# A reordered opening of an attention-plus-experts kernel: sequence 0 first on every engine, masked k by ScalarE, matmuls on the identity

## The chip, the cores and the metric

The kernel runs on one core of a Trainium2 chip. The metric is the device time of one execution in microseconds, the median of several executions. TensorE is called PE here, VectorE DVE, ScalarE ACT, GpSimd POOL and SyncE SP; SP only issues DMAs in this kernel.

## The reference

The input `x` is 32 sequences of 256 tokens with 128 features, all float32. One layer is computed:

```python
xn  = layernorm(x)                                   # no weight, no bias
qkv = (xn @ Wqkv.T)                                  # 16 heads of 8 features
q, k = rope(q), rope(k)
s   = q @ k.T / sqrt(8); s[not (j <= i and i - j <= 64)] = -inf
y   = softmax(s) @ v;  attn = y @ Wproj.T + bproj
g   = xn @ gate_w.T + gate_b; the two highest of 8 experts, softmax over the two
ffn = sum over the two of weight * (gelu(xn @ w1[e] + b1[e]) @ w2[e] + b2[e])
out = x + attn + ffn
```

## The kernel before, in words

**Units.** The 8192 tokens are 16 units of 512 tokens (`NU`); a unit is two sequences, four tiles of 128 tokens. A sequence has the number z, 0 to 31. `norm(u)` (line 259) takes a unit to its normalised rows `xn` (DVE statistics, a power of -0.5 on POOL at line 274, scaling on ACT at 283), its transposed form `xnT` (PE at 290, copied by ACT at 291) and its gate scores (PE at 295, DVE at 299).

**Rotary q and k.** `project(u, t)` (line 543) multiplies `xnT` by the weights of q (t = 0) or k (t = 1) on PE (549), and then DVE shuffles the product (558) and multiplies it by a cosine (565). The shuffled copy is multiplied by a sine, on DVE where `alone` is set (562) and on POOL otherwise (564). `sum` (569) adds the two. Since a head has only 8 features, the score matmuls work on masked copies: `km` and `qm` hold, for each of four slots, only the rows of one head in four, and zeros elsewhere. `alone(z, t)` (574) fills the copy of sequence z by four DMAs, one a slot, 32 KB each. The zeros come from `clear(n)` (499), three sets of buffers for z modulo 3; set 0 is cleared by POOL, sets 1 and 2 by ACT.

**Rounds.** The attention (`run`, line 787) goes through 32 sequences with four rounds each; "round 2.1" is round 1 of sequence 2. In a round, `high` computes scores of sequence z once (mask matmuls at 622, score matmuls at 634) and DVE takes their row maxima (648). `less` computes scores of an earlier sequence with the maxima taken off (PE at 689 and 703), and ACT exponentiates them (713). Either uses one PSUM tile, `sh` or `sl`, so the next round's `high` waits for the maximum of this one. Only `high` works in rounds 0.0 to 1.1, since `less` follows one and a half sequences behind. The four maxima of a sequence go through `parts` (659 to 662), PE (672) and ACT (677) into the rows that `less` takes off.

**Work beside.** At the end of each round `turn` advances the generator `beside` (1037) once. It hands out pieces of norms of later units, of the routing (`route`, four groups of four units, which needs the norms of its group) and of `blocks`, and it issues two scatters a turn (an indirect DMA by POOL at 457, 128 in all) of normalised rows to their experts once a group is routed. When the last scatter is out, all 71 expert blocks run in one piece (lines 909 to 1005), and the rest of the attention follows, with the experts' results added.

**Order.** The schedule is manual: each engine executes its instructions in the order in which the program issues them. SP's DMAs stand in one queue too.

**Opening.** Ahead of round 0.0, lines 868 to 906 do the norm and the projections of unit 0 by halves (half 0 is sequence 0, half 1 is sequence 1), then `weights_late` (232: transposed Wproj, the sum b2 + bproj, and its DMA to `b2_d` at 237), free the pool of raw weights (`raw.close()`, 898) and begin the norm of unit 1. `loads_late` (182) puts the loads of units 2 to 15 on SP in one go. The first act of `beside` is a memset of the tile `void` (1041) in the memory that the raw weights had, and its DMA of 910 KB (1101).

Of the kernel before, what the change touches and what calls it, by code (L numbers as in the profile page):

```python
# [11 lines left out]
F32 = mybir.dt.float32  # L12
I32 = mybir.dt.int32
BF16 = mybir.dt.bfloat16
AF = mybir.ActivationFunctionType
# [4 lines left out]
P = 128  # L20
# [3 lines left out]
T = 256  # L24
# [10 lines left out]
HB = 64  # L35
# [3 lines left out]

C_COS = 0  # L40
C_SIN = 256
C_MQ = 512
C_MK = 768
C_PICK = 960
C_PRE = 1216
C_TIE = 1344
C_NUM = 1352
C_BASE = 1360
C_RUN = C_BASE + NE
C_BLK = C_RUN + 17 * NE  # L50
C_ROW = C_BLK + NB
# [5 lines left out]
def constants():  # L57

    f = np.float32
    c = np.zeros((P, C_ALL), f)  # L60
    p = np.arange(P)
    e = np.arange(NE)
    c[:, C_PRE : C_PRE + P] = p[:, None] < p[None, :]
    c[:, C_TIE : C_TIE + NE] = NE - e
    c[:, C_NUM : C_NUM + NE] = e
    c[:, C_BLK : C_BLK + NB] = np.arange(NB)
    c[:, C_ROW : C_ROW + 128] = p[:, None] + P * np.arange(128)[None, :]
    c[:, C_BASE : C_BASE + NE] = ER * e
# [24 lines left out]
    return c, np.zeros((P, 2 * P), f)  # L93
# [3 lines left out]
def tile_layer(  # L97
# [16 lines left out]
    nc = tc.nc  # L114
# [61 lines left out]
    nc.sync.dma_start(out=wqkv_n, in_=wqkv.rearrange("(t p) c -> p t c", p=P))  # L176
    nc.sync.dma_start(out=c[:, 0:C_MQ], in_=cst[:, 0:C_MQ])
    load_x(0, slice(2, 4))
    nc.sync.dma_start(out=c[:, C_MQ:C_ALL], in_=cst[:, C_MQ:C_ALL])
    load_x(1)  # L180

    def loads_late():
        nc.sync.dma_start(out=wproj_n, in_=wproj)
        load_x(2)
        nc.sync.dma_start(out=b1_n, in_=b1)
        for u in range(3, NU):
            load_x(u)

# [25 lines left out]
    def weights(misc):  # L214

        pw = misc("pw")
        for t in range(3):
            nc.tensor.transpose(pw[:, t * D : (t + 1) * D], wqkv_n[:, t, :], ident)
        nc.vector.tensor_copy(wT[:, 2, :], pw[:, 2 * D : 3 * D])
        for t in range(2):  # L220

            natural = pw[:, t * D : (t + 1) * D].rearrange(
                "p (i s d) -> p i d s", i=4, s=4
            )
            nc.vector.tensor_copy(
                wT[:, t, :].rearrange("p (i d s) -> p i d s", i=4, d=HD), natural
            )
        pw2 = misc("pw2")
        nc.tensor.matmul(pw2[:, 0:NE], lhsT=gw_n, rhs=ident[0:NE, 0:NE], start=True, stop=True)
        nc.vector.tensor_copy(gwT, pw2[:, 0:NE])  # L230
# [16 lines left out]
    def masks():  # L247
        nc.vector.tensor_copy(
            mq, c[:, C_MQ : C_MQ + 4 * HB].rearrange("p (n k) -> p n k", n=2)
        )  # L250
        nc.vector.tensor_copy(unit2[0:HB, :], ident[0:HB, 0:HB])
        nc.vector.tensor_copy(unit2[HB:P, :], ident[HB:P, HB:P])
        nc.vector.tensor_copy(unit, ident)
        nc.vector.tensor_copy(
            pick_i, c[0:NR, C_PICK : C_PICK + 4 * HB].rearrange("p (i k) -> p i k", i=4)
        )
# [217 lines left out]
    class Attention:  # L474
# [4 lines left out]
        def __init__(self, us, pools):  # L479
            self.us = us  # L480
            self.work, self.ps_m, self.ps_y, self.ps_s, fixed = pools
            self.fixed = fixed
            self.vsts, self.kms, self.qms, self.rss = [], [], [], []
            self.qk, self.half = {}, {}
            self.seqs = {}
            self.ended = set()
            self.added = set()
            self.later = []
            self.past = []

# [8 lines left out]
        def clear(self, n):  # L499
# [11 lines left out]
            put(vst.rearrange("p n i o k -> p (n i o k)"), 1.0)  # L511
            self.vsts.append(vst)

            km = fixed.tile([P, 4, HB + T], F32, tag=f"km{n}", name=f"km{n}")
            put(km.rearrange("p s t -> p (s t)"), 0.0)
            self.kms.append(km)
            qm = fixed.tile([P, 4, T], F32, tag=f"qm{n}", name=f"qm{n}")
            put(qm.rearrange("p s t -> p (s t)"), 0.0)
            self.qms.append(qm)
# [54 lines left out]
        def alone(self, z, t, queues=(nc.sync,)):  # L574

            a = self.qk[z // 2, t][:, z % 2, :]
            to = (self.qms, self.kms)[t][z % 3]
            at = HB * t
            for s in range(4):
                queues[s % len(queues)].dma_start(  # L580
                    out=to[s::4, s, at : at + T], in_=a[s::4, :]
                )

        def v(self, z):
# [281 lines left out]


    nc.gpsimd.memset(nhalf, -0.5)
    nc.gpsimd.memset(ones, 1.0)
    att.clear(0)  # L870
    att.clear(1)

    first = [norm(0, 2 * h, 2 * h + 2) for h in range(2)]
    for h in range(2):
        for _ in range(2):
            next(first[h])
        att.flush()
    weights(misc)
    for h in range(2):
        half = slice(h, h + 1)  # L880
        next(first[h])
        next(first[h])
        for t in (1, 0):
            att.project(0, t, half, alone=h == 0)
            att.flush()
            if t or h:
                att.sum(0, t, half)
            if t and h == 0:
                att.alone(0, 1, (nc.sync, nc.scalar))
        if h == 0:  # L890
            att.sum(0, 0, half)
            loads_late()
            masks()
    for g in first:
        for _ in g:
            pass
    weights_late(misc)
    raw.close()
    nc.gpsimd.tensor_copy(
        goes[:, :, :, 0], c[:, C_ROW : C_ROW + 2 * NN].rearrange("p (k n) -> p k n", k=2)  # L900
    )
    second = norm(1)
    for _ in range(3):
        next(second)
    att.flush()
    att.clear(2)


    def experts():
# [126 lines left out]

    def beside():

        rt = early.enter_context(tc.tile_pool(name="rt", bufs=1))
        void = rt.tile([P, NE, 2, ROW], F32, tag="void", name="void")  # L1040
        nc.gpsimd.memset(void, 0.0)
# [65 lines left out]
        u, g, last = 2, 0, False  # L1107
        while next(transfers, transfers) is not transfers:
            z, r = att.now
            if (z, r) == (0, 2):  # L1110
                begin("masks0", att.masks(0))
            if (z, r) == (1, 1):
                begin("masks1", att.masks(1))

# [68 lines left out]
```

## Time and profile before

| | |
|---|---|
| median of 3 runs | 793.06 us (792.67 to 793.94) |
| profiled execution | 838.41 us |
| its span, first to last instruction | 836.6 us |
| mean granted TensorE clock | 0.976 |
| PE busy | 750.3 us of the span (90%) |
| DVE, ACT, POOL busy | 497.0, 381.9, 412.0 us |
| first maximum of round 0.0 starts | 24.62 us |
| maximum of round 2.0 starts | 63.26 us |
| experts | from 395 to about 676 us |

The profiled execution took 45 us longer than the median of the runs. In the timeline a row is: start in us, duration in us, engine, line, operation, output<-input with shapes, and how many instructions were merged; in square brackets stands how long the engine had been idle before it, and what ended that. PEld is the load of weights, which overlaps PE. A "q" behind an engine is its queue, here the issue of a DMA. In the table of stretches each pair is an engine's busy us and its instructions.

### The profile page before, as it was taken

Reading aid. Unit: us, or ns where it says so; the run is one execution under the profiler, and the core shown is the slowest. Engines: PE = TensorE matmul, PEld = TensorE weight load, DVE = VectorE, ACT = ScalarE, POOL = GpSimd, SP = SyncE. Lnnn points to the kernel's source line nnn. Section 1 sums busy time; section 2 is a strip of 40 time slices with the busy share of each in tenths; the row PEclk is TensorE's granted clock in tenths of the full one; section 3 lists DMA queues with packets and bytes.
Section 4 is the critical chain, followed back from the end, with each engine's and each line's share of the span. In section 5 each row is a group of like instructions: output and inputs, shape, how many; then the busy total and the mean of one; then the engine's idle time right before and its main releaser. Section 6 shows DMA issues by size and latency. Waiting matters only on the chain.

```text
span 836.6 us, 20453 instructions
## 1 busy us (share of the span) xinstructions
PE 750.3 (90%) x7524; PEld 483.2 (58%) x7524; DVE 497.0 (59%) x1163; ACT 381.9 (46%) x695; POOL 412.0 (49%) x668
## 2 busy tenths in 40 slices
PE   4899899888888889788999999999999989999985
PEld 2334444444444444333889998999899944444442
DVE  4658867887786687657233333333333348888763
ACT  4346455455455444434434344343344435454552
POOL 2301666477667644664355555555555553634300
PEclk9999999999999999989999999999999999999997
DMA  4600111111111111213677878887778634446100
GB/s 143 179 20 14 46 46 40 46 43 43 49 43 55 50 34 40 96 53 95 199 214 217 224 209 226 227 226 220 219 225 237 198 108 139 137 126 168 41 22 13
DMA packets 126372, 98.87 MB, mean 118 GB/s; under 512 B 14648, under 2 KB 112600, under 8 KB 126272
## 3 DMA queue, kind: packets, MB, share of 16 engines
q1 hardware_dynamic: 117344, 79.64, 34.3%
q0 software_dynamic: 8640, 17.84, 6.1%
q8 instruction: 60, 0.98, 0.5%
q14 instruction: 40, 0.33, 0.1%
q10 hardware_dynamic: 288, 0.08, 0.0%
HBM read 65.09 MB, written 24.02 MB: 107 GB/s over the span
## 4 chain that ended last, share of the span: by engine, by line
PE 63%; ACT 10%; DVE 9%; SPq 7%; issue 6%; DMA 4%; POOL 1%; ACTq 0%; DVEq 0%; POOLq 0%
PE sl L703 10%; PE ph L952 9%; PE po L970 9%; ACT pr L713 9%; PE sl L689 8%; PE sh L634 7%; PE y L725 6%; PE sh L622 5%; DVE mx L648 3%; DMA xg<-xs_d 2%; PE pm L672 2%; PE pk L549 1%; PE pq L549 1%; SPq L932 1%; PE pg L295 1%
## 5 line engine op out<-in xcount | busy, mean ns | idle before, releaser
L713 ACT ACTIVATE pr<-sl 128x1024 f32<-128x1024 f32 x128 | 130.8, 1022 | 232.2 <-PE sh L634 174.2
L648 DVE TENSOR_REDUCE mx<-sh 128x8 f32<-128x1024 f32 x128 | 156.3, 1221 | 106.0 <-PE sh L634 84.7
L981 POOL DMA_INDIRECT ys_d<-yg,at x142 | 137.3, 967 | 138.8 <-DVE yg L976 105.8
L958 ACT ACTIVATE h<-ph,b_b 128x256 f32<-128x256 f32 x284 | 116.3, 470 | 154.6 <-PE ph L952 141.6
L634 PE MATMUL sh<-km,rq 32*64 32x512 f32 x1024 | 153.4, 661 | 0.0
L457 POOL DMA_INDIRECT xs_d<-xn,slot x128 | 126.5, 988 | 44.3 <-issue 27.4
L703 PE MATMUL sl<-qm,rk 32*64 32x256 f32 (+1 forms) x1280 | 147.0, 502 | 0.0
L970 PEld LDWEIGHTS po<-w,h 128*128 128x128 f32 x1136 | 137.9, 192 | 4.3 <-issue 0.7
L970 PE MATMUL po<-w,h 128*128 128x128 f32 x1136 | 138.3, 275 | 0.6 <-issue 0.6
L952 PE MATMUL ph<-xgT,w 128*128 128x256 f32 x568 | 136.2, 383 | 1.1 <-DVE xgT L940 0.9
L689 PE MATMUL sl<-rs,pick_i 76*64 76x512 bf16 x512 | 81.9, 396 | 49.3 <-ACT pr L713 43.6
L952 PEld LDWEIGHTS ph<-xgT,w 128*128 128x128 f32 x568 | 103.3, 192 | 13.0 <-DVE xgT L940 1.1
L975 DVE TENSOR_TENSOR yg<-po,b 128x256 f32<-128x256 f32 x71 | 30.1, 424 | 112.1 <-PE pxg L938 66.4
L725 PE MATMUL y<-pr,vst 128*32 128x128 f32 (+1 forms) x1536 | 78.7, 331 | 2.8 <-issue 1.6
L689 PEld LDWEIGHTS <-pick_i 76*64 76x64 bf16 x512 | 27.8, 109 | 82.8 <-issue 71.2
L725 PEld LDWEIGHTS y<-pr,vst 128*32 128x32 f32 x1536 | 44.8, 117 | 53.3 <-issue 47.4
L703 PEld LDWEIGHTS sl<-qm,rk 32*64 32x64 f32 x1280 | 48.2, 134 | 39.2 <-issue 31.1
L677 ACT COPY rs<-pm 12x1024 bf16<-12x1024 bf16 x63 | 60.2, 1000 | 8.5 <-PE pm L672 7.9
L622 PE MATMUL sh<-mq,unit 64*64 64x512 bf16 x512 | 54.8, 417 | 3.5 <-DVE mx L648 3.2
L734 DVE STREAM_TRANSPOSE yt<-y 128x512 f32<-128x512 f32 x64 | 45.3, 708 | 10.5 <-PE y L725 9.0
L942 DVE COPY at<-xg 128x4 int32<-128x4 int32 x71 | 13.4, 189 | 62.7 <-issue 48.6
L622 PEld LDWEIGHTS <-unit 64*64 64x64 bf16 x512 | 15.7, 105 | 57.5 <-issue 57.2
(143 smaller groups left out, 840.3 us busy)
## 6 DMA issues: line engine op xcount, KB each, us to landing
w<-in_L_ffn_w_dram SPq DMA_DIRECT2D x142, 256.0 KB
xg<-xs_d SPq DMA_DIRECT2D x71, 130.0 KB
yc<-ys_d SPq DMA_DIRECT2D x32, 256.0 KB
b<-b_d SPq DMA_DIRECT2D x71, 64.0 KB
qm<-rq SPq DMA_DIRECT2D x128, 32.0 KB
out_dram<-x SPq DMA_DIRECT2D x32, 128.0 KB
km<-rk SPq DMA_DIRECT2D x126, 32.0 KB
x<-in_L_attn_x_dram SPq DMA_DIRECT2D x15, 256.0 KB
```

Of the source, the lines that this page charges most:

```text
L457: nc.gpsimd.indirect_dma_start(out=xs_d, out_offset=bass.IndirectOffsetOnAxis(ap=slot[:, n, k : k + 1], axis=0), in_=xns[n // NT][:, n % N ...
L622: nc.tensor.matmul(ps[HB * h : HB * h + HB, ii, :, :], lhsT=unit2[half, :], rhs=mq[half, which, :].unsqueeze(1).to_broadcast([HB, 4, 2 * HB]),
L634: nc.tensor.matmul(ps[HB * h : HB * h + HB, ii, :, :], lhsT=q[r, t * HB : (t + 1) * HB], rhs=km[r, :, t * HB : (t + 2) * HB], start=False, ...
L648: nc.vector.tensor_reduce(mx, ps, AX.X, ALU.max, negate=True)
L689: nc.tensor.matmul(ps[HB * e : HB * e + HB, ii, :, :], lhsT=pick_i[:, 2 * ip + ii, :], rhs=rs[e][:, :, n * P : (n + 1) * P], start=True, s ...
L703: nc.tensor.matmul(ps[HB * e : HB * e + HB, ii, :, lo:hi], lhsT=k[r, kt * HB : (kt + 1) * HB], rhs=qm[r, :, n * P + lo : n * P + hi], star ...
L713: nc.scalar.activation(pr, ps, AF.Exp, scale=1.0 / math.sqrt(HD))
L725: nc.tensor.matmul(py[32 * i : 32 * i + 32, 2 * o : 2 * o + 2, lo:hi], lhsT=self.vsts[z % 3][:, tile_, i, o, :], rhs=q["pr", n, i // 2][:, ...
L952: nc.tensor.matmul(ph[:, j * BT : (j + 1) * BT], lhsT=a[:, (k + j) * P : (k + j + 1) * P], rhs=xT, start=True, stop=True,)
L958: nc.scalar.activation(h[:, k + j, :], ph[:, j * BT : (j + 1) * BT], AF.Gelu, bias=b1_b[:, k + j, b : b + 1],)
L970: nc.tensor.matmul(po[:, n, :], lhsT=h[:, k, n * P : (n + 1) * P], rhs=z[:, k, :], start=(k == 0), stop=(k == NHC - 1),)
L981: nc.gpsimd.indirect_dma_start(out=ys_d, out_offset=bass.IndirectOffsetOnAxis(ap=at[:, n, 0:1], axis=0), in_=y[:, n, :], in_offset=None,)
```

## The change

The opening is cut in two. Ahead of the first round there is only what the scores of round 0.0 need, with the second half of unit 0 as far as its k product; the rest (the second half's q, gates, the norm of unit 1, clears, masks, late weights) becomes `opening()`, the first three turns of `beside`. The masked k of sequence 0 is written by four ACT instructions with a 0-or-1 scale per partition (`alone_first`), no longer by four DMAs, so `km` set 0 is not cleared but for its first 64 columns. Three groups of matmuls on the identity, read as bf16, with unused results are added (11, 3 and 2 of 128x512). The loads of units 2 to 15 go out one a turn from round 0.3 on. The constants come in three pieces, not two.

```diff
-C_MQ = 512
+C_HEAD = 512
+C_MQ = 516
...
+    c[:, C_HEAD : C_HEAD + 4] = (p % 4)[:, None] == np.arange(4)[None, :]
...
     load_x(0, slice(2, 4))
-    nc.sync.dma_start(out=c[:, C_MQ:C_ALL], in_=cst[:, C_MQ:C_ALL])
+    nc.sync.dma_start(out=c[:, C_MQ:C_PICK], in_=cst[:, C_MQ:C_PICK])
     load_x(1)
+    nc.sync.dma_start(out=c[:, C_PICK:C_ALL], in_=cst[:, C_PICK:C_ALL])
+    nc.sync.dma_start(out=wproj_n, in_=wproj)
 
     def loads_late():
-        nc.sync.dma_start(out=wproj_n, in_=wproj)
-        load_x(2)
-        nc.sync.dma_start(out=b1_n, in_=b1)
-        for u in range(3, NU):
+        for u in range(2, NU):
+            yield False
             load_x(u)
+            if u == 2:
+                nc.sync.dma_start(out=b1_n, in_=b1)
...
+        def alone_first(self):
+
+            a = self.qk[0, 1][:, 0, :]
+            for s in range(4):
+                nc.scalar.activation(
+                    self.kms[0][:, s, HB:], a, AF.Identity,
+                    scale=c[:, C_HEAD + s : C_HEAD + s + 1],
+                )
+
+        def warm(self, n, tag="sl"):
+
+            ps = self.ps_s.tile([P, 2, 4, P], F32, tag=tag, name=f"warm{len(self.warmed)}")
+            self.warmed.append(n)
+            some = ident.bitcast(BF16)
+            for k in range(n):
+                nc.tensor.matmul(
+                    ps[:, k % 2, :, :], lhsT=some[:, 0:P],
+                    rhs=some[:, 0:P].unsqueeze(1).to_broadcast([P, 4, P]),
+                    start=True, stop=True, skip_group_check=True,
+                )
...
     nc.gpsimd.memset(nhalf, -0.5)
-    nc.gpsimd.memset(ones, 1.0)
-    att.clear(0)
-    att.clear(1)
+    att.kms.append(fixed.tile([P, 4, HB + T], F32, tag="km0", name="km0"))
+    nc.gpsimd.memset(att.kms[0][:, :, 0:HB], 0.0)
 
     first = [norm(0, 2 * h, 2 * h + 2) for h in range(2)]
+    sides = [slice(h, h + 1) for h in range(2)]
+    att.warm(11)
     for h in range(2):
         for _ in range(2):
             next(first[h])
         att.flush()
+    next(first[0])
     weights(misc)
-    for h in range(2):
-        half = slice(h, h + 1)
-        next(first[h])
-        next(first[h])
-        for t in (1, 0):
-            att.project(0, t, half, alone=h == 0)
-            att.flush()
-            if t or h:
-                att.sum(0, t, half)
-            if t and h == 0:
-                att.alone(0, 1, (nc.sync, nc.scalar))
-        if h == 0:
-            att.sum(0, 0, half)
-            loads_late()
-            masks()
-    for g in first:
-        for _ in g:
+    att.warm(3)
+    next(first[0])
+    next(first[1])
+    att.warm(2)
+    masks()
+    att.clear(0)
+    att.project(0, 1, sides[0], alone=True)
+    att.sum(0, 1, sides[0])
+    next(first[1])
+    att.alone_first()
+    att.project(0, 0, sides[0], alone=True)
+    att.sum(0, 0, sides[0])
+    att.project(0, 1, sides[1])
+    att.flush()
+    second = norm(1)
+
+    def opening():
+
+
+        att.sum(0, 1, sides[1])
+        att.project(0, 0, sides[1])
+        att.clear(1)
+        nc.gpsimd.memset(ones, 1.0)
+        for _ in range(3):
+            next(second)
+        yield
+        att.sum(0, 0, sides[1])
+        weights_gates(misc)
+        for _ in range(2):
+            next(second)
+        for g in first:
+            for _ in g:
+                pass
+        yield
+        masks_late()
+        for _ in att.masks(0):
             pass
-    weights_late(misc)
-    raw.close()
-    nc.gpsimd.tensor_copy(
-        goes[:, :, :, 0], c[:, C_ROW : C_ROW + 2 * NN].rearrange("p (k n) -> p k n", k=2)
-    )
-    second = norm(1)
-    for _ in range(3):
-        next(second)
-    att.flush()
-    att.clear(2)
+        att.clear(2)
+        weights_late(misc)
+        nc.gpsimd.tensor_copy(
+            goes[:, :, :, 0], c[:, C_ROW : C_ROW + 2 * NN].rearrange("p (k n) -> p k n", k=2)
+        )
+        raw.close()
+        yield
...
     def beside():
 
+        yield from opening()
...
-            if (z, r) == (0, 2):
-                begin("masks0", att.masks(0))
+            if (z, r) == (0, 3):
+                begin("loads", loads_late())
```

`weights` is split too: the gate weights move to `weights_gates`, the k part is copied first, and `masks` keeps only what `high` needs (`mq` and the two 64x64 units), the rest moving to `masks_late`.

More of the change, by code (lines that the diff above doesn't have):

```diff
@@ L41 @@
 C_SIN = 256
-C_MQ = 512
[L43 to L48, printed above, removed]
+C_HEAD = 512
+C_MQ = 516
+C_MK = 772
+C_PICK = 964
+C_PRE = 1220
+C_TIE = 1348
+C_NUM = 1356
+C_BASE = 1364
 C_RUN = C_BASE + NE
@@ L218, in weights @@
             nc.tensor.transpose(pw[:, t * D : (t + 1) * D], wqkv_n[:, t, :], ident)
-        nc.vector.tensor_copy(wT[:, 2, :], pw[:, 2 * D : 3 * D])
-        for t in range(2):
+        for t in (1, 0):
             natural = pw[:, t * D : (t + 1) * D].rearrange(
@@ L227, in weights, with weights_gates @@
             )
+        nc.vector.tensor_copy(wT[:, 2, :], pw[:, 2 * D : 3 * D])
+    def weights_gates(misc):
         pw2 = misc("pw2")
@@ L252, in masks, with masks_late @@
         nc.vector.tensor_copy(unit2[HB:P, :], ident[HB:P, HB:P])
+    def masks_late():
         nc.vector.tensor_copy(unit, ident)
@@ L487, in __init__ @@
             self.added = set()
+            self.warmed = []
             self.later = []
@@ L512, in clear @@
             self.vsts.append(vst)
-            km = fixed.tile([P, 4, HB + T], F32, tag=f"km{n}", name=f"km{n}")
-            put(km.rearrange("p s t -> p (s t)"), 0.0)
-            self.kms.append(km)
+            if n > 0:
+                km = fixed.tile([P, 4, HB + T], F32, tag=f"km{n}", name=f"km{n}")
+                put(km.rearrange("p s t -> p (s t)"), 0.0)
+                self.kms.append(km)
             qm = fixed.tile([P, 4, T], F32, tag=f"qm{n}", name=f"qm{n}")
```

## The prediction

> **What bounds the kernel now.** I read first the page (spans, busy shares), then the table of stretches, then the timeline of the first 62 us, because the change touches only the opening and what the opening defers.
>
> ```profile
> span 836.6 us, 20453 instructions
> PE 750.3 (90%) x7524; PEld 483.2 (58%) x7524; DVE 497.0 (59%) x1163; ACT 381.9 (46%) x695; POOL 412.0 (49%) x668
> 0.00:56.00 56.00, 40.94 (x174) 19.91 (x174) 29.41 (x100) 22.62 (x45) 14.21 (x23) 1.00 0.46 127
> 56.00:100.00 44.00, 38.40 (x480) 18.41 (x474) 36.87 (x88) 23.99 (x40) 12.29 (x19) 1.00 0.09 27
> ```
>
> PE does 174 instructions in the first 56 us and 480 in the next 44. The opening is thin, and its PE work is slow as well:
>
> ```profile
> 9.79 0.37 ACT L291 COPY xnT<-pt 128x256 f32<-128x256 f32 x1 [0.57 <-PE pt L290]
> 15.83 0.88 ACT L283 ACTIVATE xn<-x,off,rstd 128x128 f32<-128x128 f32 x2 [5.67 <-DVE off L278]
> 16.38 0.86 PE L290 MATMUL pt<-ident,xn 128*128 128x128 f32 x2 [4.09 <-ACT xn L283]
> 22.37 1.98 PE L634 MATMUL sh<-km,rq 32*64 32x512 f32 x8
> 24.62 1.22 DVE L648 TENSOR_REDUCE mx<-sh 128x8 f32<-128x1024 f32 x1
> 31.17 1.83 POOL L1041 MEMSET void<- 128x2080 f32 x1 [5.27 <-DMA b_d<-b_n]
> 34.26 0.16 DVE L278 SCALAR_TENSOR_TENSOR off<-mv,rstd 128x4 f32<-128x4 f32 x1 [4.52 <-POOL rstd L274]
> 54.21 0.64 PE L622 MATMUL sh<-mq,unit 64*64 64x512 bf16 x4
> 58.15 0.41 PE L622 MATMUL sh<-mq,unit 64*64 64x512 bf16 x4
> 110.48 0.64 PE L622 MATMUL sh<-mq,unit 64*64 64x512 bf16 x4
> ```
>
> The reader is to see three things. Sequence 0's q and k are ready by 14.8 us, but its first scores start at 22.37, since sequence 1's half, the gates and Wproj stand ahead of them on PE and DVE. A POOL memset waits for the DMA of b2 and delays round 0.2. And the same mask matmuls take 0.64 us up to 54 us, 0.41 after 58, 0.64 once more at 110: PE has a slow and a fast clock here that the granted-clock column (1.00) does not show.
>
> The maxima start at 24.62 (round 0.0), 28.52, 36.13, 40.02, 46.11 (1.0), 51.35, 56.56 (1.2), 59.74 and 63.26 (2.0). From there the chain is continuous to the end, so a microsecond gained at 2.0 is gained at the end, unless deferred work takes it back.
>
> **Part 1: the way to the first scores.** The second half of x lands at 6.48, and DVE's statistics end at 7.59, as before. The scale `off` of sequence 0 then goes ahead of the weight copies (before: 8.16), so xn starts at 7.68. Transposes are ready for ACT by about 8.8, its copy of 0.37 ends at 9.2, and k's product takes 1.22 us in the slow rows, 0.70 at the fast ratio (0.41/0.64). DVE's four rotary steps took 11.48 to 13.16, 1.68 us: rk by 11.7. DVE's mask casts (0.29 + 2 x 0.19) lie in its wait for PE. q's steps follow on DVE, another 1.7: 13.3. Masked k: an ACT pass of 128x256 is between 0.37 (the copy above) and 0.61 (0.50 for the 128x128 scaling plus 128 elements at the 0.82 ns of the 128x768 against 128x1280 fills); I take the latter, nearest in form, pipelined at 0.49: 3 x 0.49 + 0.61 = 2.1, done by 13.85. Before, its DMAs were issued at 13.2, but nobody was waiting for them: PE's order was. Scores start at **13.85** instead of 22.37: **-8.5**.
>
> The idle matmuls stand ahead of this chain on PE. [...] The last two lie beside ACT's copy. [...]
>
> **The clock.** [...] I take fast up to the first scores, slow from there to 1.2. [...]
>
> **Part 2: the rounds to 1.2, at slow-clock durations.** First maximum at 13.85 + 1.98 + 0.27 = 16.1 (before 24.62).
> - 0.0 to 0.1: DVE has 1.22 + sum 0.4 + shuffle and product 0.8 + unit 1's statistics 1.7 = 4.1 (before 3.9): 20.2.
> - 0.1 to 0.2: unit 1's scaling waits behind the maximum on DVE: 1.9 after it starts, ACT 1.65, last transpose at +4.1, gates 1.71, masks 0.57 and scores 1.98 queued behind them on PE: 8.5. Before it was 7.6, with the b2 stall: that stall goes, and this chain is late in its place: 28.7.
> - 0.2 to 0.3: k of unit 1 2.08 and Wproj 0.47 on PE, then masks and scores: 5.1 (3.9): 33.8.
> - 0.3 to 1.0: v 1.22, gates 1.71, masks and scores: 5.3 (6.1): 39.1.
> - 1.0 to 1.1: 4.1 by PE. But unit 2's statistics now stand on DVE ahead of the maximum, and its load is behind the `void` DMA on SP: b2's DMA, 3.3 us after 0.2's maximum, needs about 2.9 more, then memset 1.83 and fill 0.2, then 910 KB (4.3 us, as at 33.3), then the load: about 13.9 us after maximum 0.2, when DVE wants it at 12.3. I take 4.4: 43.5.
> - 1.1 to 1.2: 5.2 as before: **48.7** against 56.56, **-7.9**.
>
> ACT's clears (3.1) and mask rows (2.6) lie in its idle time. POOL's q product behind the memset isn't due before 1.1.
>
> **Part 3: what comes back.** By the end of round 0.3 the order of the new program has 8 tile statistics where before had 16, so two norms move into sequences 1 and 2. By the end of sequence 2 it has 22 against 20; what it then lacks is the first routing, in sequences 3 and 4 instead of 1 to 3. Scatters start in the middle of sequence 5 (before: 3) and run at 8 a sequence to the same sequence 21; before, there were gaps in sequences 7, 8, 16 and 17. The experts start after 22.0 instead of 21.3: one round more ahead of them, one less behind. Price: sequences 2 and 3 took 14.9 us without scatters, those with scatters 16.9 with norms (183 to 318 us) and 16.9 without (318 to 386). So pieces of norms are nearly free there, and fewer gaps are paid by more rounds without scatters: 3.5 x 15.2 + 16 x 16.9 + 0.75 x 14.5 = 334.5 to the experts, against 332 plus the round more at 3.4 = 335.4. I take +0.5 for the half norm extra, between -1 and +5.
>
> Sum: -7.9 + 0.5 = -7.4 on a span of 836.6, so 829.2 us, or 831.0 for the profiled execution's 838.41. The median is 0.946 of that; scaled, -7.0: **786.0 us**.
>
> **Rivals.**
> [...]
> - **C, the load behind `void` lands late** (b2's DMA took 4.6 us from issue before, against my 2.9, and landing may add 2): 1.1 and 2.0 come some 4 us later, 789.8 us.
> - **D, slower: deferred work returns at full price.** Sequence 2's maxima (63.26 to 73.30) have no wait before them, so DVE is the bound there. Two norms at 2.1 us of DVE (4 x 0.39 + 0.5), 13 routing operations at 0.45 = 5.9 pushed into 3 and 4, and the extra round at 4.2 instead of 3.4: 4.2 + 5.9 + 0.8 = 10.9, less 7.9: +3.0 on the span, 795.9 us. It decides once more than 7.9 us come back, about three quarters of that full price. Against it: the routing's old places are free for the norms.
> - **E, nothing:** the two cancel, 793.
>
> **How the numbers follow.** Chances: mine 0.52, B 0.16, C 0.13, E 0.06, D 0.13. A measurement here can tell 0.2% (1.6 us) from no change. Faster is mine, B and C: 0.81; within 0.2% is E; slower is D. The range must leave out D and may leave out E's upper part: 779.5 (B with 2 us more) to 792.0.
>
> **What would show it.** In the new profile: first scores at 13.9, first maximum at 16.1, 0.2 at 28.7, 1.2 at 48.7, 2.0 at 55.4. Mask matmuls of 0.41 up to 14 us and 0.64 from 0.1 to 1.1 confirm the clock; 0.41 throughout means B. A DVE wait on x<-in_L_attn_x_dram in round 1.0 of 1 to 2 us is mine, of over 4 C. Experts starting less than 5 us earlier means that Part 3 is wrong; not earlier at all is D.

## The result, and the profile after

The changed kernel takes 789.85 us (median of 20 runs, 784.17 to 792.86), the kernel before 793.72 us (20 runs, 790.82 to 803.42). The ratio is 0.9926, with a 95% interval of 0.9904 to 0.9948: 0.74% faster, some 5.9 of 793.7 us. The predicted 786.0 us is a ratio of 0.9911 to the median that it started from, 793.06, and that lies inside the interval.

One thing has to be known before the two profiles are laid side by side: later runs of the same programs fall into two paces, chips on which the kernel before takes 833 to 835 us and chips on which it takes 794 to 796. On which chip the profile before (838.41 us) was taken is not on record, but it has the slower pace, and the profile after (784.24 us, span 782.5) the quicker: the stretch from the maximum of round 6.0 to that of 21.0 takes 252.0 us in the one and 222.6 in the other, and the changed kernel alone takes 255.2 us there on a slow chip (e_after) and 223.0 on a quick one (e_after_b). So the 54 us between the profiles are nearly all the chip's. Rows of the opening can still be compared: e_after and e_after_b reach the maximum of 4.0 at 87.76 and 87.79 us and that of 6.0 at 117.51 and 117.45.

The page and the table of stretches of the changed kernel, with the columns as before:

```profile
span 782.5 us, 20487 instructions
PE 729.0 (93%) x7540; PEld 473.3 (60%) x7540; DVE 500.3 (64%) x1163; ACT 382.8 (49%) x699; POOL 412.7 (53%) x668
0.00:56.00 56.00, 46.39 (x249) 17.90 (x250) 33.22 (x93) 26.95 (x54) 12.63 (x22) 0.70 0.33 94
56.00:100.00 44.00, 40.62 (x502) 20.79 (x500) 38.07 (x94) 24.86 (x42) 6.84 (x6) 1.00 0.19 57
```

PE now does 249 instructions in the first 56 us, 16 of them idle matmuls, where it did 174. The granted clock of that stretch reads 0.70 and no longer 1.00. That isn't a slower clock than before: the mask matmuls below show the same slow clock as before for most of the way. The column is discussed at the end.

The timeline of the opening, the rows that answer to those of before:

```profile
7.57 0.88 ACT L291 ACTIVATE xn<-x,off,rstd 128x128 f32<-128x128 f32 x2 [3.15 <-DVE off L286]
8.36 1.62 DVE L254 CAST mq<-c 128x256 bf16<-128x256 f32 x1
9.29 0.70 PE L559 MATMUL pk<-xnT,wT 128*128 128x256 f32 x2
11.49 0.41 PE L653 MATMUL sh<-mq,unit 64*64 64x512 bf16 x4
12.06 1.70 ACT L598 ACTIVATE km<-rk,c 128x256 f32<-128x256 f32 x4 [1.25 <-DVE rk L581]
13.86 1.93 PE L665 MATMUL sh<-km,rq 32*64 32x512 f32 x8 [1.96 <-ACT km L598]
15.84 1.23 DVE L679 TENSOR_REDUCE mx<-sh 128x8 f32<-128x1024 f32 x1 [1.53 <-PE sh L665]
17.12 0.64 PE L653 MATMUL sh<-mq,unit 64*64 64x512 bf16 x4 [0.18 <-DVE mx L679]
27.77 1.22 DVE L679 TENSOR_REDUCE mx<-sh 128x8 f32<-128x1024 f32 x1 [2.34 <-PE sh L665]
33.77 0.41 PE L653 MATMUL sh<-mq,unit 64*64 64x512 bf16 x4 [0.55 <-DVE mx L679]
34.08 1.83 POOL L1091 MEMSET void<- 128x2080 f32 x1 [2.18 <-DVE pc L690]
42.22 0.29 DVE L276 BATCH_NORM_STATS2 st<-x 128x6 f32<-128x128 f32 x1 [4.14 <-DMA x<-in_L_attn_x_dram]
49.03 0.64 PE L653 MATMUL sh<-mq,unit 64*64 64x512 bf16 x4
53.33 0.41 PE L653 MATMUL sh<-mq,unit 64*64 64x512 bf16 x4
```

The scores start at 13.86, and what they waited for last is `km` of ACT. The memset of `void` no longer waits for the DMA of b2. The clock is fast at 11.49, slow at 17.12, fast in one short stretch around 33.8, slow again, and fast once more by 53. The DVE wait for unit 2's load is 4.14 us.

The starts of the maxima in all runs are below, since nearly every reading rests on them (DVE rows of `mx`, us; "chip" is the pace of the kernel before on the chip):

```text
                      chip  scores  0.0   0.1   0.2   0.3   1.0   1.1   1.2   1.3   2.0  experts
before                 835  22.37  24.62 28.52 36.13 40.02 46.11 51.35 56.56 59.74 63.26  394.4
predicted                   13.85  16.1  20.2  28.7  33.8  39.1  43.5  48.7   -    55.4
after                  794  13.86  15.84 19.79 27.77 32.51 36.27 43.04 47.00 51.74 55.22  354.1
e0_before              835  22.09  24.34 28.23 36.69 40.58 46.67 51.91 57.07 60.24 63.74  398.0
e_after                833  13.89  15.04 18.98 26.96 31.70 36.80 42.33 46.29 49.46 53.56  388.7
e_after_b              796  14.16  16.03 19.98 27.96 32.70 36.46 43.30 47.25 51.99 55.47  354.7
e1_no_idle             835  14.15  15.30 19.24 27.22 31.96 35.02 43.04 47.00 51.74 57.22  389.0
e2_load2               835  13.77  15.33 19.27 27.25 31.99 37.09 40.99 45.95 49.12 53.22  387.9
e2_load2_b             796  14.04  15.27 19.21 27.19 31.93 37.03 40.93 46.22 49.39 53.49  357.6
e3_dma_km              835  14.81  16.23 20.17 28.15 32.89 37.99 43.41 46.99 50.16 54.27  389.1
e4_warm_rounds         833  13.66  15.56 20.92 27.22 31.13 34.88 39.97 45.97 49.14 53.24  394.1
e9_stats_early         796  13.70  15.87 19.76 25.87 30.60 35.71 39.61 44.82 47.99 52.09  356.0
e10_order_only         796  15.20  16.57 20.51 28.50 33.24 38.34 43.77 47.38 50.55 54.66  356.0
e5_before_b2first      833  22.80  25.05 28.94 32.84 39.78 45.86 51.10 56.67 61.41 66.13  395.7
e7_defer_only          833  22.66  24.90 28.79 32.69 38.69 43.23 47.13 51.84 55.01 59.12  396.8
```

### The profile page after: what moved, and what is told of

The parts are those of the page before. It is cut to its first block, busy times and chain, and to the rows that moved or that the text cites. A ratio compares the mean times of both kernels' runs of the same rounds, so it can differ in the third digit from the quotient of the medians.

```text
span 782.5 us, 20487 instructions
## 1 busy us (share of the span) xinstructions
PE 729.0 (93%) x7540; PEld 473.3 (60%) x7540; DVE 500.3 (64%) x1163; ACT 382.8 (49%) x699; POOL 412.7 (53%) x668
## 4 chain that ended last, share of the span: by engine, by line
PE 45%; ACT 4%; DVE 2%; SPq 2%; DMA 2%; issue 1%; POOL 0%; ACTq 0%; POOLq 0%
PE po L1019 16%; PE ph L1001 15%; ACT pr L744 4%; PE sl L734 3%; PE sl L720 3%; PE sh L665 2%; PE pxg L987 2%; PE y L756 2%; PE sh L653 1%; PE pm L703 1%; DMA km<-rk 0%; DMA xg<-xs_d 0%; DVE mx L679 0%; SPq L1066 0%; POOL ys_d L1030 0%
## 5 line engine op out<-in xcount | busy, mean ns | idle before, releaser
L665 PE MATMUL sh<-km,rq 32*64 32x512 f32 x1024 | 148.7, 642 | 4.6 <-DMA km<-rk 2.6
L465 POOL DMA_INDIRECT xs_d<-xn,slot x128 | 127.2, 994 | 34.7 <-issue 22.1
L734 PE MATMUL sl<-qm,rk 32*64 32x256 f32 (+1 forms) x1280 | 143.2, 486 | 0.0
L1001 PE MATMUL ph<-xgT,w 128*128 128x256 f32 x568 | 134.4, 379 | 0.0
L720 PE MATMUL sl<-rs,pick_i 76*64 76x512 bf16 x512 | 80.3, 390 | 24.3 <-ACT pr L744 19.1
L991 DVE COPY at<-xg 128x4 int32<-128x4 int32 x71 | 13.5, 190 | 102.6 <-issue 98.9
L734 PEld LDWEIGHTS sl<-qm,rk 32*64 32x64 f32 x1280 | 48.0, 131 | 37.9 <-issue 29.3
L756 PE MATMUL y<-pr,vst 128*32 128x128 f32 (+1 forms) x1536 | 69.9, 314 | 1.0 <-DVE yt L765 1.0
L756 PEld LDWEIGHTS y<-pr,vst 128*32 128x32 f32 x1536 | 40.0, 110 | 44.3 <-issue 39.0
L574 POOL TENSOR_TENSOR rotq<-rotq,c 128x512 f32<-128x512 f32 (+1 forms) x16 | 19.9, 1243 | 68.7 <-DVE rotq L568 68.5
```

Source lines behind the costliest of these rows:

```text
L465: nc.gpsimd.indirect_dma_start(out=xs_d, out_offset=bass.IndirectOffsetOnAxis(ap=slot[:, n, k : k + 1], axis=0), in_=xns[n // NT][:, n % N ...
L665: nc.tensor.matmul(ps[HB * h : HB * h + HB, ii, :, :], lhsT=q[r, t * HB : (t + 1) * HB], rhs=km[r, :, t * HB : (t + 2) * HB], start=False, ...
L720: nc.tensor.matmul(ps[HB * e : HB * e + HB, ii, :, :], lhsT=pick_i[:, 2 * ip + ii, :], rhs=rs[e][:, :, n * P : (n + 1) * P], start=True, s ...
L734: nc.tensor.matmul(ps[HB * e : HB * e + HB, ii, :, lo:hi], lhsT=k[r, kt * HB : (kt + 1) * HB], rhs=qm[r, :, n * P + lo : n * P + hi], star ...
L756: nc.tensor.matmul(py[32 * i : 32 * i + 32, 2 * o : 2 * o + 2, lo:hi], lhsT=self.vsts[z % 3][:, tile_, i, o, :], rhs=q["pr", n, i // 2][:, ...
L1001: nc.tensor.matmul(ph[:, j * BT : (j + 1) * BT], lhsT=a[:, (k + j) * P : (k + j + 1) * P], rhs=xT, start=True, stop=True,)
```

## The experiments

The theory: the reordering moves round 2.0 by some 8 us, nearly all of that reaches the end, and the idle matmuls, the load behind `void` and the way in which k is masked each weigh little. The rivals: the clock is what the change is about (B), the load takes part of the gain (C), the deferred work eats it (D). Ratios are to the kernel before on the same chip, so each can be held against the changed kernel's ratio only within the interval given.

### The two kernels again, on chips of either pace: e0_before, e_after, e_after_b

Nothing is edited. e0_before is the kernel before, the other two the changed kernel.

> The kernel before, profiled once more, since the profiled execution of before took 54 us more than that of the changed kernel while the medians differ by 4. If the change alone made that difference, the new profile is again near 836 us and the experts again take 280 us. If that execution was a disturbed one, the span is 788 to 800, round 2.0 starts near 63 us as before, and the rounds with scatters take some 14 to 15 us a sequence as in the changed kernel. It also settles what the deferred work costs: from round 2.0 to the experts' first transpose the changed kernel took 298.9 us with one round more. Deferral nearly free: before takes 294 to 298. Deferred work returning at full price: 288 or less.

> The changed kernel itself beside the kernel before on this chip, where before takes 835 us and its rounds with scatters some 17 us a sequence. My theory: what is gained lies ahead of round 2.0 and has nothing to do with the rounds with scatters, so it is again 6 to 9 us, a ratio of 0.989 to 0.993. Rival (the deferral makes those rounds denser): here, where they are slower, the gain is under 3 us, or it is over 12 us if the denser rounds help.

> The changed kernel once more, on the chip of these runs, to compare the others with. 0.986 to 0.993 of before.

Measured: e0_before 834.38 us, ratio 0.9991 (0.9965 to 1.0016); e_after 823.25 us, 0.9883 (0.9838 to 0.9928); e_after_b 789.62 us, 0.9936 (0.9914 to 0.9957). So the long profile before was no disturbed execution. Both ratios of the changed kernel lie just outside what I had expected (0.989 to 0.993, and 0.986 to 0.993), with intervals that reach into it. The table of stretches, first of e0_before and then of e_after: the opening up to the maximum of 2.0, and from there to the first transpose of the experts:

```profile
0.00:63.74 63.74, 47.07 (x242) 22.38 (x246) 33.97 (x110) 26.84 (x55) 14.22 (x23) 1.00 0.40 113
63.74:398.00 334.26, 292.41 (x3548) 142.99 (x3541) 250.54 (x579) 161.57 (x255) 196.85 (x321) 0.95 0.15 48
```

```profile
0.00:53.56 53.56, 43.63 (x230) 17.34 (x234) 32.58 (x92) 25.82 (x53) 12.62 (x22) 0.71 0.34 98
53.56:388.67 335.11, 294.62 (x3624) 145.87 (x3617) 258.43 (x604) 164.92 (x264) 197.28 (x322) 0.97 0.17 54
```

At the same pace round 2.0 comes 10.2 us earlier, and the experts 9.3 us. The second stretch is only 0.85 us longer, although it has one round more in it (3624 PE instructions against 3548). But that small sum hides large movements both ways. The same stretch in parts, from maximum to maximum (us; in the last row the scatters issued):

| | e0_before | e_after | e_after_b |
|---|---|---|---|
| 2.0 to 4.0 | 29.86 | 34.20 | 32.32 |
| 4.0 to 6.0 | 37.97 | 29.75 | 29.66 |
| 6.0 to 21.0 | 255.04 | 255.17 | 222.98 |
| 21.0 to the experts | 11.39 (three rounds) | 15.99 (four) | 14.28 (four) |
| scatters in sequences 4 and 5 | 17 | 4 | 4 |

The lead of 10.2 us at 2.0 has shrunk to 5.8 at 4.0, where the changed kernel has the statistics of 8 tiles on DVE and the kernel before those of 4; in e_after a slow stretch of the clock adds to it (last section). From 4.0 to 6.0 it grows to 14.1: scatters begin in sequence 5 and no longer in sequence 3. From there it is level over fifteen sequences, and the round more ahead of the experts takes its share at the end. So what was pushed back is not free where it lands; it is made up for two sequences later. That the later scatters are what makes sequences 4 and 5 shorter is my reading of the counts; no run takes them alone.

The experts themselves take 274.6 and 272.2 us, but two executions of the kernel before differ by 5.7 there (274.6, and 280.3 in the profile before), so nothing is read from that stretch.

### The clock: e1_no_idle, e4_warm_rounds

```diff
-    att.warm(11)
...
-    att.warm(3)
...
-    att.warm(2)
```

> The changed kernel without its three groups of idle matmuls. My theory: they only shorten the transposes and products ahead of the first scores (0.71 and 0.70 us in place of 0.86 and 1.22), so first scores come 0.5 to 0.9 us later than 13.86, and the total is 0.5 to 1 us longer, 0.1%, hardly measurable. Rival (the fast clock carries the gain): first scores and the first two rounds lose 3 us or more, total near the kernel before.

Measured: 827.94 us, 0.9879 (0.9819 to 0.9939). The timeline of PE without the idle matmuls:

```profile
9.32 1.22 PE L559 MATMUL pk<-xnT,wT 128*128 128x256 f32 x2 [0.46 <-ACT xnT L299]
12.61 0.64 PE L653 MATMUL sh<-mq,unit 64*64 64x512 bf16 x4
14.15 1.09 PE L665 MATMUL sh<-km,rq 32*64 32x512 f32 x8 [0.91 <-ACT km L598]
16.57 0.41 PE L653 MATMUL sh<-mq,unit 64*64 64x512 bf16 x4 [0.71 <-DVE mx L679]
```

The k product takes 1.22 us where the changed kernel's takes 0.70, so the idle matmuls did make the clock fast for it. But it becomes fast without them too, a little later, with nothing but the kernel's own transposes and products on PE: here the scores themselves are fast (1.09; in the profile after they took 1.93). When x lands differs by up to half a microsecond between executions, so the way to the first scores is best counted from the start of ACT's first scaling of `xn`: 6.29 to 6.30 us in all seven profiles with idle matmuls and ACT's masked k, 6.70 here (7.45 to 14.15). The idle matmuls are thus worth 0.4 us at the first scores; I had expected 0.5 to 0.9. The first maximum (15.30) lies between those of the changed kernel (15.04 to 16.03), and the ratio is that of e_after. The idle matmuls move the slow stretch; they don't take it out.

e4_warm_rounds tries to keep the clock up between rounds 0.0 and 1.1. It has the edit of e2_load2 (next), and more idle matmuls:

```diff
     (opening, round 0.0)
         for _ in range(3):
             next(second)
+        att.warm(4)
...
         weights_gates(misc)
+        att.warm(8)
...
     (beside)
             z, r = att.now
+            if (z, r) in ((0, 3), (1, 0), (1, 1)):
+                att.warm(3)
```

> The changed kernel with the load of unit 2 ahead (as in the run with that alone) and idle matmuls also in the gaps of rounds 0.0 (4), 0.1 (8), 0.3, 1.0 and 1.1 (3 each), of 512 columns. If activity keeps the fast clock, round 0.2 comes 6.5 us after 0.1 instead of 8.0, 1.0 and 1.1 follow at 3.5 each, and round 2.0 starts at 47 to 49 us instead of 53.2: 4 to 6 us more gain. Rival: such a short filling does not lift the clock, and the idle matmuls themselves, 0.43 us each at the slow one, stand ahead of real ones: round 2.0 at 54 to 57.

Measured: 822.99 us, 0.9854 (0.9804 to 0.9903), not told apart from e_after (0.9883) or e2_load2 (0.9831); the execution profiled took 827.91 us. The timeline of PE:

```profile
16.46 1.91 PE L611 MATMUL warm<-ident 128*128 128x512 bf16 x4
18.30 0.64 PE L655 MATMUL sh<-mq,unit 64*64 64x512 bf16 x4
21.31 3.26 PE L611 MATMUL warm<-ident 128*128 128x512 bf16 x8
25.73 0.41 PE L655 MATMUL sh<-mq,unit 64*64 64x512 bf16 x4
37.35 0.64 PE L655 MATMUL sh<-mq,unit 64*64 64x512 bf16 x4
```

The eight idle matmuls run mostly at the slow clock (3.26 us, 0.41 each; three take 0.81 at the fast clock, at 30.41), and a fast stretch from 25.7 to at least 32.4 follows them, where each round is one of 3.8 to 3.9 us; e2_load2_b, without the added ones, has masks of 0.64 at 24.57 and 29.27. But they stand ahead of the round's own work: the maximum of 0.1 moves from 19.27 (e2_load2) to 20.92, and after 37 the clock is slow again. By 1.0 the round is 2.2 us ahead of e2_load2's (34.88 and 37.09), and by 1.2 all of that is gone (45.97 and 45.95): two groups of three idle matmuls at the slow clock, 1.46 us at 35.96 and 1.49 at 41.70, stand ahead of the masks there. Round 2.0 comes at 53.24, e2_load2's at 53.22, where I had expected 47 to 49 and the rival 54 to 57. In this form the matmuls take what the clock gives.

### The load behind `void`: e2_load2, e2_load2_b

```diff
     nc.sync.dma_start(out=wproj_n, in_=wproj)
+    load_x(2)
...
             yield False
-            load_x(u)
             if u == 2:
                 nc.sync.dma_start(out=b1_n, in_=b1)
+            else:
+                load_x(u)
```

> The changed kernel with the load of unit 2 ahead of the DMA of the void tile on SP. DVE then no longer waits 4.1 us in round 1.0 for it. The maximum of 1.1 should start at 40.4 instead of 43.0. My theory on what is late next: PE has q of unit 1 (2.08) and the mask rows (1.06) between, which end at 43.1 in any case, so 1.2 gains only about 1.2 us (45.8 instead of 47.0), and the total 1 us. Rival: nothing else is late, and 2.6 us arrive at 2.0 and at the end.

> The changed kernel with the load of unit 2 ahead once more, next to the changed kernel on the same chip. Round 2.0 was only 0.3 us earlier with it in the profiles so far (53.2 against 53.6), since the product of q and the mask rows stand between on PE. So 0 to 0.5 us, nothing measurable. Rival: the 4 us that its ratio showed over the changed kernel's are real.

Measured: 820.64 us, 0.9831 (0.9781 to 0.9881) on a chip of 835 us, and 789.97 us, 0.9914 (0.9877 to 0.9952) on the chip of 796, where the changed kernel has 0.9936 (0.9914 to 0.9957). DVE's wait for x (2.88 us in e_after) is gone, and the maximum of 1.1 comes at 40.99 instead of 42.33 (e_after). At 2.0 only 0.3 us of that is left (53.22 and 53.56): round 1.1 to 1.2 takes 5.0 us instead of 4.0, because PE's q product and mask rows, which the changed kernel does while DVE waits, now stand inside that round. e2_load2_b is 2.0 us ahead of e_after_b at 2.0 (53.49 and 55.47); there its masks turn fast (0.41 us) at 47.8, e_after_b's only between 49.3 and 53.6. By 4.0 that lead is gone (87.67 and 87.79). In the total the two aren't told apart.

### Masked k by DMA again: e3_dma_km

```diff
-    nc.gpsimd.memset(att.kms[0][:, :, 0:HB], 0.0)
+    nc.gpsimd.memset(att.kms[0].rearrange("p s t -> p (s t)"), 0.0)
...
-    att.alone_first()
+    att.alone(0, 1, (nc.sync, nc.scalar))
```

> The changed kernel with the masked k of sequence 0 made by four DMAs again (two on SP's queue, two on ACT's) instead of four ACT instructions, its buffer cleared in full by POOL. Theory: k is ready at 12.0, the DMAs are issued until 13.3 and land about 2 us later, so the first scores start at 15.3 to 16 instead of 13.86, and 1.5 to 2 us stay to the end (0.2%). Rival (q, done at 13.6, is what binds and DMAs are as quick): 0 to 0.5 us.

Measured: 824.45 us, 0.9884 (0.9841 to 0.9928). First scores start at 14.81, 7.31 us after ACT's first scaling instead of 6.30; I had expected 1.5 to 2 us more. ACT's passes are worth 1.0 us at the first scores, and the total doesn't show it.

### Order alone: e10_order_only

The edits of e1_no_idle and e3_dma_km together: what is left of the change is its order, with the work that it puts back, and its spread loads.

> The changed kernel without idle matmuls and with DMAs for the masked k: what is left of the change is the order on the engines, with the work that it puts into the first rounds and behind. Theory (the order is the change): first scores at 14.8 to 15.6, total within 0.2% of the changed kernel's. Rival (either part hides the loss of the other when taken out alone): first scores at 16 or later and a ratio to before near 0.993 to 0.997, halfway back.

Measured: 792.28 us, 0.9957 (0.9933 to 0.9981). First scores at 15.20, 7.71 us after ACT's first scaling: 1.4 more than the changed kernel's 6.3, the sum of the two parts taken out (0.4 and 1.0). In the kernel before it was 14.0 us, so the order gives 6.3 of the 7.7 us by which this way got shorter. Round 2.0 comes at 54.66. By its rows the order alone brings 2.0 from 63.26 (before) to 54.66, as far as the whole change does (55.22 in the profile after, 55.47 in e_after_b). By the totals it gives 0.43% of the 0.64% that the changed kernel has on the same chip; the two intervals overlap, so whether the other two parts add anything to the total stays open. The first scores came where the theory had them (14.8 to 15.6), the ratio where the rival had it (0.993 to 0.997).

### The b2 stall alone: e5_before_b2first

The kernel before, with its loads of units 4 to 15 taken out of `loads_late` and issued after `weights_late(misc)`, so that the DMA of b2 no longer stands behind them:

```diff
         nc.sync.dma_start(out=b1_n, in_=b1)
-        for u in range(3, NU):
-            load_x(u)
+        load_x(3)
+
+    def loads_rest():
+        for u in range(4, NU):
+            load_x(u)
...
     weights_late(misc)
+    loads_rest()
     raw.close()
```

> The kernel before with the loads of units 4 to 15 issued behind the small DMA of b2 on SP instead of ahead of it. POOL's memset of void then has no 5.3 us wait, and the maximum of round 0.2 starts at 32.5 to 33.5 instead of 36.1. Theory: some 3 us of that reach round 2.0 and the end, as nothing else is late there. Rival: the void DMA and the masked k of sequence 1 now stand behind twelve loads, and the wait only moves to round 1.0, 0 us.

Measured: 833.77 us, 0.9992 (0.9964 to 1.002). Its timeline:

```profile
32.70 2.08 PE L552 MATMUL pk<-xnT,wT 128*128 128x512 f32 x2
32.84 1.23 DVE L651 TENSOR_REDUCE mx<-sh 128x8 f32<-128x1024 f32 x1 [0.80 <-PE sh L637]
34.57 1.72 PE L298 MATMUL pg<-gwT,xnT 128*128 128x8 f32 x8
36.13 1.09 PE L293 MATMUL pt<-ident,xn 128*128 128x128 f32 x4
37.16 0.64 PE L625 MATMUL sh<-mq,unit 64*64 64x512 bf16 x4
39.78 1.22 DVE L651 TENSOR_REDUCE mx<-sh 128x8 f32<-128x1024 f32 x1 [2.86 <-PE sh L637]
```

Round 0.2 comes 3.9 us earlier than in e0_before (32.84 and 36.69), and one round later 0.8 us of that are left (39.78 and 40.58). PE is late in its place: the k product of unit 1, gates and transposes, which in e0_before run from 32.0 on while DVE waits for the scale behind the memset, now stand between the scores of 0.2 and those of 0.3. The rival's delay on the SP queue isn't there: the DMAs of `km` and `qm` of sequence 1 are issued at 34.0 and 37.9, in e0_before at 34.3 and 37.7. At 2.0 this run is even 2.4 us later (66.13 and 63.74), as its masks are still slow at 58.7 and 63.4, where e0_before's turned fast by 58.7 (0.41 us), and its rounds from 1.2 to 2.0 take 4.7 us each, e0_before's 3.2 and 3.5; that part goes with the clock, and nothing shows that the edit brings it. The stall taken out by itself is replaced by the next.

### Deferral alone: e7_defer_only

The kernel before with `room`, the number of pieces of work beside in the rounds of sequence 0, at zero: `((0, 0, 0, 0) if z == 0` in place of `((2, 2, 0, 0) if z == 0`.

> The kernel before with its opening, but with the norms of units 2 and 3 moved out of rounds 0.0 and 0.1 into sequences 1 and 2, as the change does it (DVE's order from round 1.0 on is the changed kernel's). This is the deferral alone. Theory (nearly free): round 0.2 no longer waits for the scale of unit 2 (4.5 us), so round 2.0 starts 3 to 5 us earlier, the stretch from there to the experts gets longer by the one round more only, and the total is 2 to 5 us shorter. Rival (deferred work returns at full price): some 8 to 10 us come back, and the total is 3 to 6 us longer than before.

Measured: 829.18 us, 0.9974 (0.9948 to 1.0). Its stretches:

```profile
0.00:59.12 59.12, 40.98 (x214) 17.76 (x218) 29.60 (x93) 24.42 (x49) 13.27 (x22) 1.00 0.43 122
59.12:396.81 337.69, 295.78 (x3624) 146.97 (x3616) 257.73 (x604) 165.13 (x264) 197.37 (x322) 0.97 0.15 47
```

Round 2.0 comes 4.6 us earlier than in e0_before, and the stretch to the experts is 3.4 us longer (337.69 against 334.26), about the price of the one round more that is now in it. That round is then missing after the experts (157.5 us, against 164.3). Inside the stretch the course is that of e_after again: the lead of 4.6 us is 0.3 at 4.0 and 7.1 at 6.0. So the deferred norms do come back at about their price in sequences 2 and 3, as rival D had it (with a slow stretch of the clock in it here too, masks of 0.64 at 76.1), and what D left out, the shorter sequences 4 and 5, makes up for them.

### What sets 0.1 to 0.2: e9_stats_early

The edit of e2_load2, and the statistics and the scale of unit 1 ahead of round 0.0:

```diff
     second = norm(1)
+    for _ in range(3):
+        next(second)
+    att.flush()
```

with as many pieces fewer in the first two turns of `opening`.

> The changed kernel with the load of unit 2 ahead, and the statistics of unit 1 on DVE ahead of the maximum of round 0.0 instead of behind it, so that its rows are scaled and ready before the maximum of 0.1. Theory (0.1 to 0.2 takes 8.0 us because scale, ACT's scaling, transposes and gates stand in a row behind that maximum and ahead of 0.2's scores on PE): the maximum of 0.0 up to 1 us later, 0.2 at 24.5 to 25 instead of 27.0, and 2 to 2.5 us arrive at 2.0 and at the end, 0.3%. Rival (something behind it, such as the weights of the gates or PE's slow clock, binds as well): less than 1 us.

Measured: 787.11 us, 0.9919 (0.9886 to 0.9952), the lowest median on its chip. The timeline of the changed kernel (ACT's scaling of unit 1), and then of this one (the same, and the maximum of 0.2 that waits for it):

```profile
21.54 1.65 ACT L291 ACTIVATE xn<-x,off,rstd 128x128 f32<-128x128 f32 x4 [4.94 <-DVE off L286]
```

```profile
18.64 1.65 ACT L293 ACTIVATE xn<-x,off,rstd 128x128 f32<-128x128 f32 x4 [2.20 <-DVE off L288]
25.87 1.23 DVE L681 TENSOR_REDUCE mx<-sh 128x8 f32<-128x1024 f32 x1 [2.34 <-PE sh L667]
```

The scaling starts 2.9 us earlier, and 0.1 to 0.2 takes 6.1 us instead of 8.0. The statistics delay the first maximum by 0.6 us against e2_load2_b; so 0.2 comes 1.3 us earlier (25.87 and 27.19; I had expected 24.5 to 25), and 2.0 1.4 us earlier (52.09 and 53.49; I had expected 2 to 2.5). So the chain that the prediction named does bind, for 1.9 of its 8.0 us; what binds after that was not looked for. The 1.4 us are still there at 4.0 (86.26 and 87.67). In the total the gain isn't clear of e2_load2_b (0.9914) nor of the changed kernel (0.9936), and e_after_b's profile reaches the experts sooner than this one (354.7 and 356.0).

## Why the prediction was right, step by step

- **The way to the first scores** was right to 0.01 us in the profile after, partly by luck. Masked k took 1.70 us and not 2.1, but DVE's cast of `mq` took 1.62 us and not 0.29; and the landing of x moves the scores between 13.86 and 14.16 from one execution to the next. The order gave most of it: 15.20 in e10_order_only against 22.1 to 22.4 before.
- **Idle matmuls:** the sum has no time for them, and that was right: they lie in the wait for x. In the profile after the three groups take 4.87, 1.05 and 0.59 us of PE, and k's product starts 1.72 us after ACT's first scaling (7.57 to 9.29); in e1_no_idle, without them, 1.87 us after it (7.45 to 9.32). The sum takes this product at the fast 0.70 us. What makes the clock fast there no row of before shows; the runs showed 0.70 with the idle matmuls and 1.22 without (e1_no_idle). But there the clock becomes fast too, with the kernel's own transposes and products, and the first scores come 0.4 us later.
- **The clock, and rival B.** Slow in thin rounds was right: 0.64 at 17.1, 44.3 and 49.0. So B, the clock fast throughout, falls. A busy PE was not always fast: it was busy for 5.93 and 8.00 us of the stretches of 8 us from 16 and from 24 (shown in the last section), with masks of 0.64 at 17.1, 25.2 and 29.9. In the profile before it was busy for all of the 15.90 us from 39.9 to 55.8, with masks of 0.64 at 43.5, 48.7 and 54.2. What turns the clock, no run here shows. What the prediction didn't have were single fast stretches, as at 33.8 in the profile after and e_after_b, not in e_after. They shift rounds by 1.3 us (0.3 to 1.0 takes 3.76 us in the profile after, 5.10 in e_after). Nor did it have the single slow stretches after 2.0 (last section).
- **0.1 to 0.2, the chain of unit 1's norm:** 8.5 predicted, 8.0 measured in all runs of the changed kernel; e9_stats_early shows that it is this chain. That taking out the b2 stall by itself gains nothing, e5_before_b2first shows.
- **Unit 2's load, and rival C.** The term was mis-sized: 1.0 to 1.1 took 5.5 (e_after) to 6.8 us (after), not 4.4. DVE's wait was 4.14 us, where I had put over 4 as the sign of C. Rival C's number, 789.8 us, is also nearer to the measured 789.85 than my 786.0. But C's loss did not come with the wait: C had 1.1 and 2.0 some 4 us later than mine, and they came at 43.04 and 55.22, for my 43.5 and 55.4. The wait is long because 1.0 was early, in the profile after by the fast stretch: 1.1 comes at 43.04 there and in e1_no_idle, whose 1.0 came 1.2 us earlier. And PE's q product and mask rows run meanwhile, so that 1.1 to 1.2 took 4.0 us and not 5.2. The sign was badly chosen: a wait tells how early the waiting engine is, as much as how late the transfer.
- **Part 3, the deferred work:** the term was +0.5 us, with the round more ahead of the experts (put at 3.4) set against the one less behind. Counted like that, the stretch of e_after costs -2.5 us against e0_before (335.11 - 334.26 - 3.4) and +0.6 against the profile before (331.09), so the term is right within what two profiles of one kernel differ by. Its parts were less right: 2.0 to 4.0 was to take 30.4 us and took 32.3 to 34.2 in the changed kernel, so the piece of rival D that has norms return at their price there came true in the main: without a slow stretch it is 2.5 us for the one norm more that stands there, and D had put a norm at 2.1. What the prediction had right is that the scatters, begun later and without gaps, need no more sequences (6.0 to 21.0: 255.0 and 255.2 us). Rival D's sum falls by that, and by the totals of e_after and e7_defer_only.
- **The sum:** the terms' errors went both ways, and 2.0 came at 53.6 to 55.5, for 55.4 predicted. The premise that a microsecond gained at 2.0 is gained at the end did not hold as it stood: e_after and e_after_b are 1.9 us apart at 2.0 and 0.03 at 4.0. The sum was -7.4 us on the span. At the pace of the profile before it was -9.7 us of 832.5 (ratio 0.9883, so 6.0 to 13.5 by its interval), at the pace of the timed runs -5.1 to -5.9. The prediction scaled the one to the other by 0.946, which these ratios neither bear out nor refute. No profile of the kernel before was taken on a quicker chip, so where a microsecond or two might go there stays open.

## What to carry to other kernels

Where several engines stand idle at the start of a kernel, look for the one chain that leads to the first result and put it ahead in every engine's order; that order was worth most here. What it pushes back is not free where it lands (two sequences took 2.5 to 4.3 us longer), so follow the lead through the whole kernel: 10.2 us at 2.0, 5.8 at 4.0, 14.1 at 6.0, 9.3 at the experts. Removing one stall alone gave nothing (e5_before_b2first): ask of every stall what is late right behind it. And judge a wait by the round after it, not by its length: e_after's wait for x of 2.88 us cost 0.3 us at 2.0, since the other engine did its work meanwhile.

## What was not expected of the hardware

- **The granted-clock column.** In the first stretch before it read 1.00 while the mask matmuls took 0.64 us; after, it reads 0.50 and 0.56 with the same 0.64:

```profile
16.00:24.00 8.00, 5.93 (x23) 2.58 (x24) 5.33 (x18) 2.49 (x6) 2.17 (x3) 0.50 0.11 34
24.00:32.00 8.00, 8.00 (x35) 3.01 (x36) 3.82 (x8) 5.63 (x12) 1.27 (x1) 0.56 0.01 2
```

  The runs are consistent with a column that is right only from the first change to the slow clock on: it reads 1.00 in the openings of e0_before and e7_defer_only, whose masks took 0.64 us throughout up to 54.8 and 50.0 us. Durations of one instruction of fixed shape are the safer clock.
- **Slow stretches come and go in one program.** e2_load2 and e2_load2_b are the same program. Their masks of round 3.0, the first from e2_load2:

```profile
69.44 0.41 PE L655 MATMUL sh<-mq,unit 64*64 64x512 bf16 x4
69.86 0.64 PE L655 MATMUL sh<-mq,unit 64*64 64x512 bf16 x4
```

  In the four profiles with this one slow stretch (e_after, e2_load2_b, e4_warm_rounds, e9_stats_early; 0.57 to 0.64 us) 2.0 to 4.0 takes 34.2 us, in five without it (after, e_after_b, e2_load2, e3_dma_km, e10_order_only) 32.3 to 32.7 (e1_no_idle, whose masks are slow at 54.5 instead, has 33.1). On the quick chip, 10.0 to 12.0 takes 35.4 us with masks of 0.64 at 193 to 195 (e2_load2_b, e9_stats_early) and 32.5 without. So one slow stretch goes with 1.5 to 2.9 us, and two single profiles that differ by 2 us at one round don't tell two kernels apart.
- **DVE casts beside POOL.** A cast of 128x32 to bf16 takes 0.24 us (median of 32), but 1.73 beside the `void` memset (34.08 to 35.91, shown above):

```profile
34.27 1.73 DVE L692 CAST pc<-rest 128x32 bf16<-128x32 f32 x1
```

  It ends with the memset, at 36.00. `mq`'s cast, 1.62 us instead of 0.29, does the same with the memsets of `vst` and `qm`, 8.19 to 9.83. In e1_no_idle the first of these casts ends before the memset begins (33.72, and 34.10) and takes 0.23 us. Why a cast lasts as long as the memset beside it, no run here shows; these rows put the price at the whole rest of the memset.
- **Chips differ.** The same program takes 794 us on one chip and 835 on another. DVE's maxima last 1.22 us on both, and e_after and e_after_b are level at 4.0 and at 6.0. Of the 36 us by which they differ between 2.0 and the experts (335.1 and 299.2), 32 lie between 6.0 and 21.0, where the scatters run. Over the whole stretch PE is busy for 294.6 and 280.0 us, at a granted clock of 0.97 and 1.00. So some 21 of the 36 us are time in which PE waits, and why the waits are longer there, no run here shows.
